# A fixed TensorE order by kind of product in the attention of a decoder layer, with folded maxima

## The chip, the core and the metric

The kernel runs on one core of a Trainium2 chip. A core has a matrix engine (TensorE, in profiles PE, with its weight loads as PEld), a vector engine (VectorE, DVE), a scalar engine for activations (ScalarE, ACT), a general engine (GpSimd, POOL) and a queue engine that issues DMAs (SyncE, SP). Each works through its own list of instructions in the order in which the program was built, and waits on semaphores for the others. TensorE writes its products to a memory of its own, PSUM, that is divided into banks; DVE and ACT read them from there. Everything else is in SBUF or in DRAM.

The metric is the device time of one execution in microseconds. A profile is one such execution, recorded instruction by instruction.

## What is computed

One decoder layer on x of shape (16, 256, 256): pre-norm self-attention with 16 heads of 16 channels, pre-norm mLSTM cross attention with 8 heads of 32 channels against a context, and a mixture of experts (top 2 of 8). Cut to what matters here:

```
h = layernorm(x)
qkv = einsum('bsd,ndh->bnsh', h, W_qkv);  q, k, v = split(qkv, 3)
attn = softmax(q k^T / sqrt(16) + causal mask);  out = attn v
x = x + einsum('bds,nhd->bsd', out.reshape(B, 256, S), W_out)     # a reordering with a scale

q = layernorm(x);  k = v = ctx                                    # mLSTM
pre = 15 tanh((concat(q, k, v) @ ifgate_w.T + ifgate_b) / 15)
log_d = cumulated log_sigmoid(forget) differences + input gate, causal
d = exp(log_d - rowmax(log_d))
s = (q k^T / sqrt(32)) * d
h = s v / (max(|rowsum(s)|, exp(-m)) + 5e-5)
x = x + rms_normed(h) * gain

h = layernorm(x)
probs = softmax(h @ router_w + router_b);  two experts a token
x = x + sum over the two of  prob * gelu(h @ up_e^T) @ down_e^T
```

All data is float32.

## The kernel before

**Attention.** It goes through 16 sequences b, each in four quads of four heads: a round k = 4 b + quad. For a round:

- `maxima(k)`: eight row-group products (a contraction of 16 channels, one head in each group of 32 rows of TensorE's array) put the scores into two PSUM tiles of two banks, `ps_s`. The DVE subtracts the causal mask's blocks (`less`, line 371), takes the maxima of the rest (`off`, 375), reduces `less` (376), joins `off` (377) and transposes (380). Four small DMAs write the row maxima into a spare row of `qt`, so that the next product subtracts them.
- `weights(k)`: eight row-group products with a contraction of 32 give the shifted, transposed scores in two more such tiles, `ps_st` (398, 402); ACT exponentiates them into `p` (406), POOL zeroes the upper triangle (341).
- `values(k)`: eight column-group products (the heads lie beside each other in the output's partitions, 417, 422) into `ps_av`; ACT copies it to `avt`.
- by sequence: `start1` (layer norm on DVE, ACT and POOL), `turn1` (four transposes, whole array), `project` twice and `project_v` (whole array, 309 and 329), `by_token` (eight transposes into two tiles `ps_o`, 435, which the DVE scales into `av`, 440 to 442).

`attend_next(k)` calls maxima(k), turn1 or a projection of the next sequence, weights(k - 2), values(k - 4), project_v, by_token, start1. The tiles of maxima, weights and of the mLSTM's scores share one pool of three pairs of banks, `ps_p`; everything else of whole-array and column-group products shares two single banks, `ps_t`.

**The mLSTM beside it.** From round k0 = 36 on, when eight sequences are through, `take_evenly` calls between two rounds some five steps of a list that `mixing(0, False)` and `reorder(0)` made: `gather` and `spread` (transposes that reorder the attention's output), `load2`, `start2`, `turn2` (transposes of context and x), `gates` (32 column-group products, then a chain on ACT and DVE), `gates_by_token` (transposes of its result), `maxima2`, `decay` (ACT's exponentials, POOL's triangle), `scores2` (row groups into `ps_p`, the DVE multiplies by `d`, 618), `values2` (column groups, 632), `finish` (transposes and the norm), `layer3`, `scale3`, `turn3`, `logits`, `softmax3`, `choose`, `count`, and `send`, POOL's scatter of rows to the experts' table.

**What sets the order.** Up to the experts, a scheduler puts each engine's instructions in order by a model of their times when the program is built; the calls above only give their priorities. It splits groups: where it thinks that a slot is not free yet, it takes a product from another group first. The experts' part, from line 1187 on, stands under `tc.manual_schedule(engines={PE, ACT, SP})`, where those engines keep the order of the calls; the second half of the mLSTM is interleaved there by the same steps.

Of the kernel before, what the change touches and what calls it, by code (L numbers as in the profile page):

```python
# [12 lines left out]
F32 = mybir.dt.float32  # L13
# [7 lines left out]
P = 128  # L21
# [8 lines left out]
GB = 8  # L30
# [39 lines left out]
def decoder_layer(  # L70
# [35 lines left out]
    def xtile(b, c):  # L106
# [15 lines left out]
        out=mask_a, in_=mask_a, compare_op=ALU.is_ge, fill=1e10, base=0,  # L122
        pattern=[[0, SC], [-1, P]], channel_multiplier=1,
    )
    gain = const.tile([P, D], F32, name="gain")
    wrout_sb = const.tile([P, DC, E], F32, name="wrout_sb")
    brout_sb = const.tile([P, E], F32, name="brout_sb")
# [32 lines left out]
    def statistics(b, mv, rstd):  # L160

        for c in range(SC):
            st = lstm.tile([P, 6], F32, tag="st", name="st", bufs=4)
            nc.vector.bn_stats(st, xtile(b, c))
            nc.vector.bn_aggr(mv[:, c, :], st)
        nc.vector.tensor_scalar(rstd, mv[:, :, 1], LN_EPS, None, ALU.add)
        nc.scalar.activation(rstd, rstd, AF.Ln)
        nc.scalar.activation(rstd, rstd, AF.Exp, scale=-0.5)

    def normalized(xn, b, mv, rstd, engine=nc.gpsimd):  # L170
# [103 lines left out]
            nc.vector.tensor_reduce(wq[:, c, :], wsel, AX.X, ALU.add)  # L274

    def step(f, *args):
        return lambda: f(*args)

# [67 lines left out]
    def maxima(k):  # L346

        b, quad = divmod(k, NQ)
        qt, kt, mx = seq[b]["qt"], ks[b % 2], mxs[k % 2]

        ps = [ps_p.tile([P, 2, 512], F32, tag="s", name="ps_s") for _ in range(2)]

        def channels(h):
            return slice(HP * h, HP * h + HA)

        for h in range(4):
            nc.tensor.matmul(  # L357
                ps[h // 2][:, h % 2, P : P + S], lhsT=qt[channels(h), quad, P:], rhs=kt[channels(h), quad, :],
                start=True, stop=True,
            )  # L360
        for h in range(4):
            nc.tensor.matmul(  # L362
                ps[h // 2][:, h % 2, :P], lhsT=qt[channels(h), quad, :P], rhs=kt[channels(h), quad, :P],
                start=True, stop=True,
            )

        less = att.tile([P, 4, SC, P], F32, tag="less", name="less", bufs=1)
        off = att.tile([P, 4], F32, tag="off", name="off")
        for j, p in enumerate(ps):
            part = slice(2 * j, 2 * j + 2)  # L370
            nc.vector.tensor_tensor(  # L371
                less[:, part], mask_a[:, None].to_broadcast([P, 2, SC, P]),
                p.rearrange("p h (c k) -> p h c k", c=SC)[:, :, :, :P], ALU.subtract,
            )
            nc.vector.tensor_reduce(off[:, part], p[:, :, P:S], AX.X, ALU.max)  # L375
        nc.vector.tensor_reduce(mx[:, :, :4].rearrange("p c h -> p h c"), less, AX.X, ALU.min)  # L376
# [32 lines left out]
    def values(k):  # L409

        b, quad = divmod(k, NQ)
        p, v = quads[k]["p"], vs[b % 2]
        if quad == 0:
            seq[b]["avt"] = att.tile([P, NQ, S], F32, tag="avt", name="avt", bufs=1)
# [12 lines left out]
        del quads[k]  # L427
# [550 lines left out]

    avs = {}

    def attend_next(k):
# [12 lines left out]
        if 0 <= k - 4 < B * NQ:  # L994
            done, part = divmod(k - 4, NQ)
            if done % GB == 0 and part == 0:
                avs[done // GB] = big.tile([P, SC, HA, GB, NA], F32, tag="av", name="av")
            values(k - 4)
        if b + 1 < B and quad == NQ - 1:
            project_v(b + 1)  # L1000
        if 0 <= k - 4 < B * NQ and part == NQ - 1:
            by_token(done)
        if quad == NQ - 2 and b + 2 < B:
            start1(b + 2)

    for b in range(2):
        start1(b)
    turn1(0)
    for i in range(2):
        project(0, i)  # L1010
    project_v(0)
    output_sums()
    nc.vector.tensor_scalar(gain, gain, 1.0, None, ALU.add)
    k0 = GB * NQ + 4
    last = B * NQ + 4

# [33 lines left out]
    gathers, spreads = reorder(1)  # L1050
    for f in gathers:
        f()
    attention.close()
    singles.append(ctx.enter_context(tc.tile_pool(name="ps_s", bufs=6, space=PSUM)))

# [215 lines left out]
```

## Time and profile before

| | us |
|---|---|
| three executions: median | 1269.7 |
| lowest, highest | 1261.93, 1269.94 |
| the profiled execution | 1278.24 |
| its span, first to last instruction | 1276.5 |

Its mean granted TensorE clock is 0.906 of full speed. The costliest groups are the experts' products (lines 1140 and 1158, 271.1 and 265.5 us); of the attention, in microseconds of busy time:

| line | engine, what | count | busy | mean ns |
|---|---|---|---|---|
| 357 | PE, maxima, 256 columns | 512 | 84.0 | 443 |
| 398 | PE, weights, 256 columns | 512 | 79.3 | 462 |
| 309 | PE, project | 256 | 71.7 | 428 |
| 371 | DVE, less | 128 | 86.9 | 679 |
| 375 | DVE, off | 128 | 53.3 | 417 |
| 376 | DVE, reduce | 64 | 77.6 | 1212 |
| 618 | DVE, scores times d | 96 | 60.3 | 683 |
| 406 | ACT, exponential | 128 | 98.7 | 810 |
| 341 | POOL, triangle of p | 128 | 78.7 | 639 |

How to read it: the time of a PE row is the modelled time from a product's start to its end, and products of different row or column groups run beside each other, so their busy times overlap; the pitch, from the start of one group to that of the next, is what counts. Each float32 product of the program is two records. "[0.56 <-DVE off L375]" behind a row means that the engine was idle for 0.56 us before it, until the DVE's instruction of line 375 released it. The granted clock is the share of full TensorE speed that the chip's throttle gave.

### The profile page before, as it was taken

The numbers are of one execution on the slowest core, as the hardware profiler recorded it, in microseconds if no ns is written. First come the engines' busy times: TensorE is split into PE (matmuls) and PEld (weight loads), VectorE is DVE, ScalarE is ACT, GpSimd is POOL, SyncE is SP. The second block draws the span as 40 slices with busy tenths as digits, with TensorE's granted clock in tenths as the row PEclk, the third lists the DMA queues.
The fourth block names the chain that finished last, engine by engine and source line by source line (L and its number), as shares of the span: only waits on it lengthen the run. The fifth ranks groups of instructions, "written<-read, shape, count | busy, mean of one in ns | idle before, by whom it ended". The sixth has DMA issues, their size and how long they took to land. (4 is left out here: it accounts for less than half of the span.)

```text
span 1276.5 us, 23870 instructions
## 1 busy us (share of the span) xinstructions
PE 1137.2 (89%) x8962; PEld 879.5 (69%) x8962; DVE 611.9 (48%) x1660; ACT 460.6 (36%) x934; POOL 400.8 (31%) x449
## 2 busy tenths in 40 slices
PE   5999999989889998665898879999899999999993
PEld 4677777646656555344676647877678999999992
DVE  4788777767667557253458544564411111111110
ACT  2344444336546453122575316633211111111110
POOL 5233332345433334614121053201732112221121
PEclk9699999879889787686899969999979999999997
DMA  5200000003112100243675536635569788888825
GB/s 183 60 15 17 13 17 13 10 10 138 31 38 98 43 18 18 96 173 125 232 244 167 183 114 216 195 120 163 166 208 375 238 267 270 267 264 271 272 55 148
DMA packets 63410, 177.14 MB, mean 139 GB/s; under 512 B 11776, under 2 KB 43520, under 8 KB 48128
## 3 DMA queue, kind: packets, MB, share of 16 engines
q1 hardware_dynamic: 49072, 155.75, 35.0%
q0 software_dynamic: 13680, 19.08, 7.4%
q8 instruction: 72, 1.18, 0.4%
q10 hardware_dynamic: 544, 0.79, 0.2%
q14 instruction: 42, 0.34, 0.1%
HBM read 147.19 MB, written 28.13 MB: 137 GB/s over the span
## 5 line engine op out<-in xcount | busy, mean ns | idle before, releaser
L1140 PE MATMUL ps_u<-xt,up 128*128 128x128 f32 (+1 forms) x1632 | 271.1, 323 | 5.9 <-issue 4.2
L1158 PE MATMUL ps_d<-down,h 128*128 128x256 f32 x1136 | 265.5, 389 | 3.8 <-issue 3.4
L1140 PEld LDWEIGHTS ps_u<-xt,up 128*128 128x128 f32 x1632 | 240.3, 194 | 32.0 <-issue 11.4
L1158 PEld LDWEIGHTS ps_d<-down,h 128*128 128x128 f32 x1136 | 216.9, 195 | 38.8 <-issue 10.4
L1163 POOL DMA_INDIRECT acc<-y,to x71 | 110.2, 1553 | 392.9 <-DVE y L1162 316.1
L1146 ACT ACTIVATE h<-ps_u 128x512 f32<-128x512 f32 x84 | 50.2, 597 | 248.8 <-PE ps_u L1140 213.2
L341 POOL TENSOR_SCALAR_AFFINE_SELECT p<-p 128x512 f32<-128x512 f32 x128 | 78.7, 639 | 191.1 <-ACT p L406 146.3
L406 ACT ACTIVATE p<-ps_st 128x768 f32<-128x768 f32 x128 | 98.7, 810 | 91.8 <-PE ps_st L402 89.6
L371 DVE TENSOR_TENSOR less<-mask_a,ps_s 128x512 f32<-128x512 f32 x128 | 86.9, 679 | 43.3 <-PE ps_s L362 43.2
L1120 DVE COPY xt<-ps_r 128x256 f32<-128x256 f32 (+1 forms) x51 | 26.9, 527 | 145.4 <-PE ps_r L1118 126.5
L357 PE MATMUL ps_s<-kt,qt 16*128 16x256 f32 x512 | 84.0, 443 | 10.2 <-DVE d L618 6.3
L398 PE MATMUL ps_st<-qt,kt 32*128 32x256 f32 x512 | 79.3, 462 | 13.9 <-DVE off L375 12.7
L1162 DVE TENSOR_SCALAR y<-ps_d,wt 128x256 f32<-128x256 f32 x71 | 34.0, 478 | 110.0 <-PE ps_d L1158 95.3
L813 POOL DMA_INDIRECT table<-x,place x64 | 63.5, 991 | 64.3 <-DVE place L809 19.6
L376 DVE TENSOR_REDUCE mxs<-less 128x8 f32<-128x1024 f32 x64 | 77.6, 1212 | 0.0
L309 PE MATMUL ps_qk<-xnt,wqk_sb 128*128 128x256 f32 x256 | 71.7, 428 | 5.6 <-DVE wg_in L488 2.7
L341 POOL TENSOR_SCALAR_AFFINE_SELECT d<-d 128x512 f32<-128x512 f32 x64 | 40.6, 681 | 105.6 <-ACT d L600 90.0
L172 POOL TENSOR_SCALAR xn<-x,mv,rstd 128x256 f32<-128x256 f32 x46 | 56.6, 1240 | 43.7 <-PE ps_t L181 27.8
L618 DVE SCALAR_TENSOR_TENSOR d<-ps_sc,d 128x384 f32<-128x384 f32 (+1 forms) x96 | 60.3, 683 | 14.8 <-PE ps_sc L613 7.4
L600 ACT ACTIVATE d<-mb,at 128x256 f32<-128x256 f32 x128 | 63.8, 499 | 9.6 <-DMA mb<-mm 9.6
L1148 DVE COPY h<-ps_u 128x512 f32<-128x512 f32 x58 | 39.8, 688 | 52.0 <-PE ps_u L1140 34.1
L309 PEld LDWEIGHTS ps_qk<-xnt,wqk_sb 128*128 128x128 f32 x256 | 51.2, 210 | 17.5 <-issue 3.6
(220 smaller groups left out, 1652.8 us busy)
## 6 DMA issues: line engine op xcount, KB each, us to landing
up<-in_wup SPq DMA_DIRECT2D x51, 1024.0 KB
down<-in_wdown SPq DMA_DIRECT2D x51, 1024.0 KB
mb<-mm SPq DMA_DIRECT2D x16, 1024.0 KB
rows<-table SPq DMA_DIRECT2D x20, 265.0 KB
rows<-table SPq DMA_DIRECT2D x31, 132.5 KB
x<-in_x SPq DMA_DIRECT2D x16, 256.0 KB
kt<-qt SPq DMA_DIRECT2D x128, 32.0 KB
qt<-rowed SPq DMA_DIRECT2D x256, 1.0 KB
```

Of the source, the lines that this page charges most:

```text
L309: nc.tensor.matmul(ps[:, i, :], lhsT=wqk_sb[:, dc, n : n + 4].rearrange("p n j h -> p (n j h)"), rhs=xnt[:, dc, :], start=dc == 0, stop=dc ...
L341: nc.gpsimd.affine_select(out=block, in_=block, compare_op=ALU.is_ge, fill=0.0, base=0, pattern=[[0, 4], [1, P]], channel_multiplier=-1,)
L357: nc.tensor.matmul(ps[h // 2][:, h % 2, P : P + S], lhsT=qt[channels(h), quad, P:], rhs=kt[channels(h), quad, :], start=True, stop=True,)
L371: nc.vector.tensor_tensor(less[:, part], mask_a[:, None].to_broadcast([P, 2, SC, P]), p.rearrange("p h (c k) -> p h c k", c=SC)[:, :, :, : ...
L376: nc.vector.tensor_reduce(mx[:, :, :4].rearrange("p c h -> p h c"), less, AX.X, ALU.min)
L398: nc.tensor.matmul(ps[h][:, :S], lhsT=kt[rows(h), quad, :P], rhs=qt[rows(h), quad, :], start=True, stop=True)
L406: nc.scalar.activation(p[:, part, :], x_, AF.Exp, scale=1.0 / math.sqrt(HA))
L600: nc.scalar.activation(d[:, h, :S], mb[:, n, :], AF.Exp, bias=at[:, 0, j, n : n + 1], scale=-1.0)
L813: i = nc.gpsimd.indirect_dma_start(out=table, out_offset=bass.IndirectOffsetOnAxis(ap=place, axis=0), in_=row, in_offset=None, bounds_chec ...
L1140: nc.tensor.matmul(ps[:, j, :], lhsT=m["up"][:, dc, f * P : (f + 1) * P], rhs=m["xt"][:, dc, :t], start=dc == 0, stop=dc == DC - 1,)
L1158: nc.tensor.matmul(ps, lhsT=m["h"][:, f, c * P : (c + 1) * P], rhs=m["down"][:, f, :], start=f == 0, stop=f == FC - 1)
L1163: a = nc.gpsimd.indirect_dma_start(out=acc, out_offset=bass.IndirectOffsetOnAxis(ap=m["to"][:, c : c + 1], axis=0), in_=y, in_offset=None, ...
```

## The change

It does five things.

1. `attend_next` no longer calls the work at once. It sorts it into four slots: 0 holds maxima (row groups) and the mLSTM's loads, norms, `maxima2`, `decay` and `scores2`; 1 holds the whole-array products (turn1, project, project_v, by_token) and those steps that have no place of their own; 2 holds weights (row groups); 3 holds values (column groups) with `values2`, `gates`, `logits`, `layer3`, `scale3`. The steps of a sequence stay in their order, as do the steps that belong to none. The slots are then called one after the other.
2. The attention, from its first step on, stands under `tc.manual_schedule(engines={PE})`: TensorE keeps the order of the calls. The other engines are still ordered by the scheduler. The mLSTM's steps of a round are handed to `attend_next` with it instead of being called behind it.
3. values runs three rounds behind maxima instead of four; project_v and by_token come ahead of weights; `start1` is called one quad earlier.
4. In `maxima`, the block behind the diagonal is no longer reduced to `off`; a scalar_tensor_tensor folds it into `less` (min of -p and less), and the one reduce that follows covers it.
5. The layer norms' epsilon is added as the bias of ACT's logarithm instead of by a DVE operation (48 of them), and the context's transposes in `turn2` are copied from PSUM by ACT instead of the DVE.

The diff, cut to its core:

```diff
@@ statistics
-        nc.vector.tensor_scalar(rstd, mv[:, :, 1], LN_EPS, None, ALU.add)
-        nc.scalar.activation(rstd, rstd, AF.Ln)
+        nc.scalar.activation(rstd, mv[:, :, 1], AF.Ln, bias=ln_eps[:, 0:1])
@@ maxima
-            nc.vector.tensor_reduce(off[:, part], p[:, :, P:S], AX.X, ALU.max)
+            nc.vector.scalar_tensor_tensor(
+                less[:, part, 1], p[:, :, P:S], -1.0, less[:, part, 1], ALU.mult, ALU.min
+            )
         nc.vector.tensor_reduce(mx[:, :, :4].rearrange("p c h -> p h c"), less, AX.X, ALU.min)
-        nc.vector.scalar_tensor_tensor(mx[:, 1, :4], off, -1.0, mx[:, 1, :4], ALU.mult, ALU.min)
@@ turn2
-        nc.vector.tensor_copy(m["ct"], ps)
+        nc.scalar.copy(m["ct"], ps)
@@ attend_next
+    def attend_next(k, also=()):
+        slots = [[], [], [], []]
         b, quad = divmod(k, NQ)
         if k < B * NQ:
-            maxima(k)
+            slots[0].append(step(maxima, k))
         if b + 1 < B:
             if quad == 0:
-                turn1(b + 1)
+                slots[1].append(step(turn1, b + 1))
             elif quad < NQ - 1:
-                project(b + 1, quad - 1)
+                slots[1].append(step(project, b + 1, quad - 1))
+            else:
+                slots[1].append(step(project_v, b + 1))
+        if quad == NQ - 1 and 0 < b <= B:
+            slots[1].append(step(by_token, b - 1))
+        if quad == 1 and b + 2 < B:
+            slots[0].append(step(start1, b + 2))
         if 0 <= k - 2 < B * NQ:
-            weights(k - 2)
+            slots[2].append(step(weights, k - 2))
...
+        if 0 <= k - 3 < B * NQ:
+            slots[3].append(step(values, k - 3))
+        at, least = {}, 0
+        for f, *args in also:
+            own = 1
+            if f in (load2, start2, maxima2, decay, scores2):
+                own = 0
+            elif f in (values2, logits, gates, layer3, scale3):
+                own = 3
+            if f in by_sequence:
+                own = at[args[0]] = max(own, least, at.get(args[0], 0))
+            else:
+                own = least = max([own, least, *at.values()])
+            slots[own].append(step(f, *args))
+        for f in sum(slots, []):
+            f()
@@ the loops
-    for k in range(k0):
-        attend_next(k)
+    with tc.manual_schedule(engines={PE}):
+        ...
+        for k in range(k0):
+            attend_next(k)
...
-    for k in range(k0, last):
-        attend_next(k)
-        take_evenly(steps, k + 1 - k0, last - k0 - EARLY)
+    with tc.manual_schedule(engines={PE}):
+        for k in range(k0, last):
+            done = min(all_steps, all_steps * (k + 1 - k0) // (last - k0 - EARLY))
+            n = max(0, done - (all_steps - len(steps)))
+            attend_next(k, [f.work for f in steps[:n] if f is not None])
+            steps = steps[n:]
```

More of the change, by code (lines that the diff above doesn't have):

```diff
@@ L124, in decoder_layer @@
     )
+    ln_eps = const.tile([P, 1], F32, name="ln_eps")
+    nc.gpsimd.memset(ln_eps, LN_EPS)
     gain = const.tile([P, D], F32, name="gain")
@@ L276, in step, with run @@
     def step(f, *args):
-        return lambda: f(*args)
+        def run():
+            f(*args)
+        run.work = f, *args
+        return run
     seq, quads = {}, {}
@@ L367, in maxima @@
         less = att.tile([P, 4, SC, P], F32, tag="less", name="less", bufs=1)
-        off = att.tile([P, 4], F32, tag="off", name="off")
         for j, p in enumerate(ps):
@@ L413, in values @@
         if quad == 0:
+            if b % GB == 0:
+                avs[b // GB] = big.tile([P, SC, HA, GB, NA], F32, tag="av", name="av")
             seq[b]["avt"] = att.tile([P, NQ, S], F32, tag="avt", name="avt", bufs=1)
@@ L979, in decoder_layer @@
     avs = {}
-    def attend_next(k):
+    def attend_next(k, also=()):
+        slots = [[], [], [], []]
         b, quad = divmod(k, NQ)
         if k < B * NQ:
-            maxima(k)
+            slots[0].append(step(maxima, k))
         if b + 1 < B:
             if quad == 0:
-                turn1(b + 1)
+                slots[1].append(step(turn1, b + 1))
             elif quad < NQ - 1:
-                project(b + 1, quad - 1)
-        if 0 <= k - 2 < B * NQ:
-            weights(k - 2)
[L994 to L1013, printed above, removed]
+                slots[1].append(step(project, b + 1, quad - 1))
[5 more added lines that the diff above has]
+            slots[0].append(step(start1, b + 2))
+        if 0 <= k - 2 < B * NQ:
+            slots[2].append(step(weights, k - 2))
[15 more added lines that the diff above has]
+            f()
+    by_sequence = (load2, start2, turn2, maxima2, decay, scores2, values2, finish, layer3, scale3, turn3, logits)
     k0 = GB * NQ + 4
@@ L1025, in take_evenly @@
             take(steps)
-    for k in range(k0):
-        attend_next(k)
+    with tc.manual_schedule(engines={PE}):
+        for b in range(2):
+            start1(b)
+        turn1(0)
+        for i in range(2):
+            project(0, i)
+        project_v(0)
+        output_sums()
+        nc.vector.tensor_scalar(gain, gain, 1.0, None, ALU.add)
+        for k in range(k0):
+            attend_next(k)
     tail = NBLK - THIRD
@@ L1046, in decoder_layer @@
     all_steps = len(steps)
-    for k in range(k0, last):
-        attend_next(k)
-        take_evenly(steps, k + 1 - k0, last - k0 - EARLY)
-    gathers, spreads = reorder(1)
-    for f in gathers:
-        f()
+    with tc.manual_schedule(engines={PE}):
[4 more added lines that the diff above has]
+            steps = steps[n:]
+        gathers, spreads = reorder(1)
+        for f in gathers:
+            f()
     attention.close()
```

## The prediction, made before the changed kernel ran

> **What bounds the kernel now.** I read the page first, then the windows by stage, then TensorE's timeline in one period of each stage, then the DVE's beside it.
>
> From the page:
>
> ```profile
> span 1276.5 us, 23870 instructions
> PE 1137.2 (89%) x8962; PEld 879.5 (69%) x8962; DVE 611.9 (48%) x1660; ACT 460.6 (36%) x934; POOL 400.8 (31%) x449
> PE   5999999989889998665898879999899999999993
> PEclk9699999879889787686899969999979999999997
> ```
>
> TensorE is the busy engine from slice 2 to the end, but its granted clock sags in the middle. By stage (columns: window, length, busy of PE, PEld, DVE, ACT, POOL, clock, DMA share, GB/s):
>
> ```profile
> 67.00:250.00 183.00, 175.92 (x1956) 129.59 (x1948) 141.14 (x317) 83.28 (x152) 56.82 (x80) 0.99 0.06 14
> 250.00:500.00 250.00, 229.06 (x2276) 146.72 (x2274) 162.07 (x360) 129.04 (x319) 105.35 (x126) 0.86 0.15 49
> 500.00:546.00 46.00, 32.20 (x231) 20.66 (x232) 17.88 (x82) 10.38 (x25) 25.37 (x28) 0.57 0.24 83
> 546.00:940.00 394.00, 333.42 (x2313) 258.01 (x2312) 202.44 (x618) 164.69 (x312) 116.88 (x116) 0.89 0.52 174
> ```
>
> The plain attention (67 to 250) is bound by TensorE at full clock. The mixed stage (attention with the mLSTM, 250 to 500) has 20.9 us of idle TensorE and, at 0.86, loses about 0.14 x 250 = 35 us to the clock. Behind 546 the order is written out by hand already; what happens earlier shifts it as a whole. The change acts before 546.
>
> TensorE in one plain period, quads 3 and 0:
>
> ```profile
> 104.39 0.88 PE L357 MATMUL ps_s<-kt,qt 16*128 16x256 f32 x8
> 105.27 0.70 PE L398 MATMUL ps_st<-qt,kt 32*128 32x256 f32 x4
> 106.53 0.48 PE L398 MATMUL ps_st<-qt,kt 32*128 32x256 f32 x2 [0.56 <-DVE off L375]
> ...
> 110.00 0.60 PE L435 MATMUL ps_o<-ident,avt 128*128 128x128 f32 x4
> 110.53 0.69 PE L357 MATMUL ps_s<-kt,qt 16*128 16x256 f32 x2
> 111.15 0.66 PE L435 MATMUL ps_o<-ident,avt 128*128 128x128 f32 x4
> ```
>
> Two losses are seen: `weights` finds the third PSUM pair only, and waits for the DVE to empty the first pair of `maxima`; and one row-group product alone between two groups of transposes takes 111.15 - 110.53 = 0.62 us, where eight together take 0.88. The DVE at that time:
>
> ```profile
> 105.36 0.69 DVE L371 TENSOR_TENSOR less<-mask_a,ps_s 128x512 f32<-128x512 f32 x1 [1.00 <-PE ps_s L362]
> 105.97 0.42 DVE L375 TENSOR_REDUCE off<-ps_s 128x2 f32<-128x256 f32 x1
> 106.30 0.68 DVE L371 TENSOR_TENSOR less<-mask_a,ps_s 128x512 f32<-128x512 f32 x1
> 107.23 1.21 DVE L376 TENSOR_REDUCE mxs<-less 128x8 f32<-128x1024 f32 x1
> ```
>
> **The change, part by part.** Pitches (start to start, full clock) from this timeline: maxima 0.9, half a projection 1.92, `project_v` 1.83, four transposes 0.55 to 0.6, weights 0.87, values 0.78.
>
> *Plain stage.* Quads 1 and 2 keep their order: 4.5 us each (115.58 to 120.08), no change. Quad 3 with quad 0 now takes 115.58 - 104.39 = 11.19 us. New order: maxima, `project_v`, eight transposes, weights, values; then maxima, four transposes, weights, values. In the built order the DVE works less, less, fold, fold, reduce. A fold is an operation the trace lacks on this tile; its nearest rows are the reduce it replaces (0.42) and the scalar_tensor_tensor on 128x384 of ps_sc (0.55), so 0.42. The first PSUM pair is then free 0.60 + 0.60 + 0.42 + 0.14 = 1.8 us after maxima, not 1.25. Quad 3: `project_v` and the transposes (3.3 us, with 0.3 for ACT to empty ps_v) hide that; but values needs the slot of the first ps_o, which the DVE empties only behind its maxima work: less and fold 1.95, reduce 1.24, reciprocal 0.29, transpose 0.26, product 0.21, the second reciprocal 0.29, `av` 0.60, semaphore 0.14: 5.0 us after maxima, where TensorE is there at 3.3 + 0.87 = 4.17. Quad 3 is 0.95 + 5.0 + 0.79 = 6.75. Quad 0: four transposes do not cover 1.8 us, so weights ends 1.8 + 0.85 (106.53 to 107.38, what follows the wait) after maxima: 0.95 + 2.65 + 0.79 = 4.4. Sum 11.15 against 11.19: the wait of 0.56 and the lone product are gone, and two waits on the DVE take their place. Nine sequences: 0 us at full clock. The folded maxima save the DVE a 0.17 us operation and its 0.04 gap a round: off the path.
>
> *Mixed stage, removed.* About 25 lone products as at 110.53, 0.62 - 0.11 each: -12.5 us. Waits of weights for the DVE (12.7 us between 20 and 520, nine of 0.56 in the plain stage): -8.
>
> *Mixed stage, added.* `scores2` now follows maxima at once, both row groups, three PSUM pairs for four: its second half waits for the DVE's fold, 1.8 us instead of 0.3: about 1.5 us, 14 times, +21, less the 6 us that maxima now waits for `d`: +15. Three rounds have two sets of scores, and the second waits also for the first `d` behind the reduce (4.3 us after maxima; 0.95 us a `d`): +2 each, +6. In four quad-3 rounds `finish` follows the transposes of `by_token` and waits for both ps_o slots: +6 in all; values behind ps_o in the others, +3. `gates`: from its last product (277.45) to the transposes of its rows (286.04) the chain on ACT and DVE, a reciprocal of 3.35 us in it, takes 8.6 us; now 2.9 us of products stand between, and TensorE holds weights, values and everything behind: +3, the second unit +1. `count`: logits' transpose at 499.84, its product at 509.16, with 1.9 us idle; nothing stands between any more: +5. Sum of the stage: -20.5 + 39 = +18.
>
> *Values one round sooner.* weights, two exponentials (1.5), two selections on POOL (1.22): 3 us, with 3.2 to 5.7 us until values. POOL's other pieces are 2.4 us. I put 0; if POOL stands in the way in a third of 28 rounds, +10. *Order of sums, start:* maxima of quad 0 no longer stand behind the second sequence's projection and its 2.66 us of waiting for wg_in: -2 (0 to -5). *eps as bias:* 48 DVE operations of 0.21 us gone, off TensorE's path in the attention; *ct on ACT* (0.58 instead of 0.69 us on the DVE): in the mixed stage ACT is busy 129 of 250 us and empties in turn, 0.1 us a transpose; behind 546 TensorE waits 11.6 us for the DVE's ct, 10.8 of it once, and ACT could stand behind a gelu instead. Both together -2 (-8 to +6).
>
> *The clock.* A row speaks against the new waits:
>
> ```profile
> 238.57 0.60 PE L398 MATMUL ps_st<-qt,kt 32*128 32x256 f32 x2 [0.98 <-DVE off L375]
> ...
> 241.39 2.39 PE L329 MATMUL ps_v<-wv_sb,xnt 128*128 128x256 f32 x8
> ```
>
> After an idle 0.98 us the same product runs at half speed (2.39 for 1.99, 0.70 for 0.41) for some 4 us, so such a gap costs 2 us more; gaps of 0.77 (415.11) and 0.76 (476.75) do the same, nine gaps of 0.56 never did. The Trainium skill ("TensorE: Matmul & The Clock Gate", "Why this matters for your kernels") asks only that gaps stay under about 3 us; by it no new wait but those of gates and count costs clock, and the sum is +14. By the row, the gap before values in quad 3 (0.76 in the trace's way of counting) may cost 2 us in each of nine sequences: half of them, +9, of which I take +5; in the mixed stage I let new gaps and removed ones cancel. I follow the row. Sum: 0 + 5 + 18 - 2 - 2 = +19 us.
>
> The profiled execution took 1278.2 us (span 1276.5 and 1.7 around it), 0.7% above the median of 1269.7; I add the sum to the median: **1288 us**.
>
> **The rivals.**
> 1. *Faster: the clock stays up.* Place: 250 to 500. With four blocks a round, TensorE may see no short gaps, and most of the 35 us of clock comes back beside the lone products' 12.5. For: nine of the eleven falls that the timeline shows between 260 and 500 follow a wait of a row-group product for the DVE. Against: scores behind maxima. It decides from a clock of 0.95 in that stage on (0.09 x 250 = 22 us back): -12.5 - 22 = -35: 1235 and lower.
> 2. *No change: the stage follows its chain of evacuations.* DVE's 5.3 us for a maxima and a scores set, and ACT beside it, set the rounds before and after: removed and added waits are equal: 1270.
> 3. *Much slower: the clock falls in every round.* Each 1.5 us gap before scores costs 2 us more (14 x 2), and both waits in all nine plain sequences (36): 1288 + 28 + 31 = about 1345 at the most, 1315 by half.
> 4. *POOL holds values:* +10, 1298; the lag is what it needs.
> 5. *The order is not what TensorE gets:* excluded, the built program has it.
>
> **How the numbers follow.** Forecast with rival 4: 0.46 (1275 to 1305); rival 3: 0.10; rival 2: 0.19; rival 1: 0.25. Less than 1% (12.7 us) is about what a measurement can tell from no change. Faster by over 1%: 0.25; within: 0.20, some of the forecast's lower end among it; slower: 0.55. The range reaches into rival 1 and rival 3: 1235 to 1318; the slower cases alone 1275 to 1318.
>
> **What would show it.** Right: quads 3 and 0 together near 11.1 us, with TensorE waiting for a fold in quad 0 and for the DVE's `av` in quad 3; waits of `scores2` for folds of over 1 us, a dozen of them; a wait of 4 us or more behind gates and behind the logits' transposes; mixed stage 15 to 20 us longer at a clock of 0.8 to 0.88. Wrong: clock of the mixed stage at 0.95; lone-product savings with no wait before scores; values waiting for POOL as the longest wait; or a gain or loss of over 10 us behind the attention.

## The result and the profile after

| | before | after |
|---|---|---|
| median of six executions each, us | 1269.09 (1261.93 to 1272.76) | 1333.84 (1332.1 to 1340.39) |
| span of the profiled one, us | 1276.5 | 1331.9 |
| its mean granted TensorE clock | 0.906 | 0.889 |

The ratio of the medians is 1.0524, with a 95% interval of 1.0489 to 1.0559. The forecast was 1288: the sign was right, the size (+19 us) was a third of what came (+65), and the time lies above the range, which reached to 1318.

The page of the kernel after, the lines that answer to those shown of before:

```profile
span 1331.9 us, 23756 instructions
...
PE 1112.4 (84%) x8962; PEld 876.2 (66%) x8962; DVE 582.2 (44%) x1532; ACT 474.6 (36%) x950; POOL 400.0 (30%) x450
...
PE   5989999767777767656589887999989999999993
...
PEclk8999999766887878768689887999979999999997
```

TensorE's busy time is 24.8 us *less* than before (1137.2), at a lower mean clock. The loss is idle TensorE, 84% busy for 89%, and it stands in slices 8 to 17, of 33 us each. By stage (columns as before; the windows are moved with the stages, the last two by 56 us):

```profile
67.00:243.00 176.00, 164.13 (x1887) 122.72 (x1885) 127.93 (x267) 80.24 (x144) 53.25 (x76) 0.98 0.07 14
243.00:556.00 313.00, 221.30 (x2269) 151.50 (x2264) 155.86 (x342) 136.24 (x331) 110.75 (x130) 0.78 0.12 40
556.00:602.00 46.00, 31.98 (x245) 20.41 (x246) 12.69 (x53) 11.38 (x23) 23.21 (x26) 0.61 0.22 77
602.00:996.00 394.00, 332.00 (x2317) 258.84 (x2316) 195.74 (x594) 170.75 (x320) 116.81 (x116) 0.89 0.53 173
```

In the mixed stage TensorE is busy 221 us of 313; before it was 229 of 250. Where the time went, by the first and last starts that the trace gives for each tile:

| us | before | after | difference |
|---|---|---|---|
| start to the first transposition of `turn2` | 251.7 | 243.7 | -8.0 |
| from there to the last maxima (mixed stage) | 250.0 | 320.5 | +70.5 |
| from there to the experts' first product | 66.0 | 60.8 | -5.2 |
| from there to the last one's start | 677.2 | 675.0 | -2.2 |

The second milestone does not stand at quite the same place in both: in round 40 `turn2` comes 6.4 us behind the start of the maxima before, and 1.6 us after. So some 5 us of the -8.0 and of the +70.5 are this shift alone.

Two places of the mixed stage, TensorE's timeline and then VectorE's. First a set of scores behind maxima:

```profile
355.33 0.71 PE L362 MATMUL ps_s<-kt,qt 16*128 16x256 f32 x8
...
356.08 0.60 PE L616 MATMUL ps_sc<-qt,ct 32*128 32x256 f32 x4
360.19 0.48 PE L616 MATMUL ps_sc<-qt,ct 32*128 32x256 f32 x2 [3.51 <-DVE less L379]
...
361.05 1.11 PE L182 MATMUL ps_t<-ident,xn 128*128 128x128 f32 x4
```

```profile
353.14 0.69 DVE L678 TENSOR_TENSOR sq<-ps_hn,g 128x512 f32<-128x512 f32 x1 [1.03 <-ACT g L677]
357.58 0.75 DVE L166 BATCH_NORM_STATS2 st<-x 128x6 f32<-128x256 f32 x2 [3.74 <-POOL x L682]
...
358.46 1.25 DVE L375 TENSOR_TENSOR less<-mask_a,ps_s 128x512 f32<-128x512 f32 x2
359.63 0.75 DVE L379 SCALAR_TENSOR_TENSOR less<-ps_s,less 128x256 f32<-128x256 f32 x2
```

The second half of `scores2` waits 3.51 us for the fold of line 379. That fold is not late because it is long. In VectorE's queue the statistics of the next layer norm (line 166) stand ahead of `less`, and they wait 3.74 us for GpSimd to finish the mLSTM's `x`. TensorE was through with these maxima by 356.3, but their banks come free only at about 360.

Then the end of the stage, where the experts' rows are counted:

```profile
556.02 0.69 PE L802 MATMUL ps_n<-sel,earlier 128*128 128x64 f32 x2 [9.63 <-DVE sel L789]
556.50 3.10 PE L802 MATMUL ps_n<-sel,ones 128*128 128x56 f32 x14
...
559.96 1.24 PE L403 MATMUL ps_st<-qt,kt 32*128 32x256 f32 x8
...
561.55 1.08 PE L424 MATMUL ps_av<-p,v 128*32 128x256 f32 x8
```

TensorE stands for 9.63 us in front of `count`, while VectorE works through the choice of experts; weights, values and the next maxima, which need nothing of it, are queued behind. Afterwards the clock is at half: eight records of weights take 1.24 us, not 0.71.

### The profile page after: what moved, and what is told of

The parts are those of the page before. It is cut to its first block, busy times and chain, and to the rows that moved or that the text cites. A ratio compares the mean times of both kernels' runs of the same rounds, so it can differ in the third digit from the quotient of the medians.

```text
span 1331.9 us, 23756 instructions
## 1 busy us (share of the span) xinstructions
PE 1112.4 (84%) x8962; PEld 876.2 (66%) x8962; DVE 582.2 (44%) x1532; ACT 474.6 (36%) x950; POOL 400.0 (30%) x450
## 5 line engine op out<-in xcount | busy, mean ns | idle before, releaser
L1184 PE MATMUL ps_d<-down,h 128*128 128x256 f32 x1136 | 262.0, 386 | 4.3 <-issue 4.1
L375 DVE TENSOR_TENSOR less<-mask_a,ps_s 128x512 f32<-128x512 f32 x128 | 82.1, 681 | 114.7 <-PE ps_s L367 113.6
L314 PE MATMUL ps_qk<-xnt,wqk_sb 128*128 128x256 f32 x256 | 82.9, 481 | 0.7 <-ACT xnt L301 0.7
L362 PE MATMUL ps_s<-kt,qt 16*128 16x256 f32 x512 | 61.0, 448 | 15.8 <-ACT p L411 9.5
L607 ACT ACTIVATE d<-mb,at 128x256 f32<-128x256 f32 x128 | 63.6, 497 | 18.8 <-DMA mb<-mm 14.5
L314 PEld LDWEIGHTS ps_qk<-xnt,wqk_sb 128*128 128x128 f32 x256 | 58.2, 238 | 14.9 <-issue 1.5
L403 PE MATMUL ps_st<-qt,kt 32*128 32x256 f32 x512 | 63.0, 495 | 4.3 <-DVE less L379 3.9
L616 PE MATMUL ps_sc<-qt,ct 32*128 32x256 f32 x256 | 38.1, 475 | 33.2 <-DVE less L379 22.4
L625 DVE SCALAR_TENSOR_TENSOR d<-ps_sc,d 128x384 f32<-128x384 f32 (+1 forms) x96 | 60.6, 677 | 11.6 <-POOL d L346 8.6
```

The costliest lines, as they stand in the source:

```text
L314: nc.tensor.matmul(ps[:, i, :], lhsT=wqk_sb[:, dc, n : n + 4].rearrange("p n j h -> p (n j h)"), rhs=xnt[:, dc, :], start=dc == 0, stop=dc ...
L362: nc.tensor.matmul(ps[h // 2][:, h % 2, P : P + S], lhsT=qt[channels(h), quad, P:], rhs=kt[channels(h), quad, :], start=True, stop=True,)
L375: nc.vector.tensor_tensor(less[:, part], mask_a[:, None].to_broadcast([P, 2, SC, P]), p.rearrange("p h (c k) -> p h c k", c=SC)[:, :, :, : ...
L403: nc.tensor.matmul(ps[h][:, :S], lhsT=kt[rows(h), quad, :P], rhs=qt[rows(h), quad, :], start=True, stop=True)
L607: nc.scalar.activation(d[:, h, :S], mb[:, n, :], AF.Exp, bias=at[:, 0, j, n : n + 1], scale=-1.0)
L1184: nc.tensor.matmul(ps, lhsT=m["h"][:, f, c * P : (c + 1) * P], rhs=m["down"][:, f, :], start=f == 0, stop=f == FC - 1)
```

## The experiments

The executions were taken on several chips. On some the kernel before takes about 1268 us, on others about 1229, nearly all of the difference behind the experts' first product (677 and 636 us from there). So each run is read by its ratio to the kernel before on its own chip, and by the lengths of its stages. An expectation in microseconds that was written for 1269 is read by its difference from before.

**The edits apart.** Four kernels: the small edits without the order, the order without the small edits, and two that give the mixed stage's TensorE back to the scheduler.

```diff
 small_alone: before, with folded maxima, bias=ln_eps, and nc.scalar.copy(m["ct"], ps)
 order_alone: after, with those three taken back
 mixed_by_scheduler: after, with
-    with tc.manual_schedule(engines={PE}):
+    if True:
         for k in range(k0, last):
 plain_fixed_only: after, with
+    for k in range(k0, last):
+        attend_next(k)
+        take_evenly(steps, k + 1 - k0, last - k0 - EARLY)
```

> The kernel before with only the three small edits (folded maxima, LN's constant as ScalarE's bias, turn2's ct copied by ScalarE) and TensorE's order left to the scheduler. Theory A (the added time is TensorE's fixed order in the mixed stage, which waits for evacuations that VectorE and ScalarE reach late): within 8 us of before, 1262 to 1277. Theory B (the small edits did it: first half of the maxima's banks freed 0.6 us later, ScalarE loaded with more): 1300 or more.

> The changed kernel with the three small edits taken back: only the order is fixed (values a round earlier with it). Theory A: the cost stays, 1320 to 1345 (the folded maxima shorten VectorE's chain by about 0.7 us in 26 rounds of the mixed stage at most, so undoing them may add up to 15). Theory B: 1290 or less.

> The changed kernel, but the mixed stage is not under TensorE's fixed order: the steps are called in the same slots and the scheduler orders TensorE as it did before. Theory A (the fixed order itself, which cannot move scores2 or a transposition behind other work when its bank is not free): 1260 to 1285, the first count 45 us or more after the mixed stage's start earlier than in the changed kernel. Theory C (the order in which the slots call the steps is what costs, since the scheduler of the other engines follows it too): 1315 or more.

> The changed kernel up to round 36 (fixed order, which reached the mixed stage 8 us before the kernel before did); in the mixed stage the steps are dealt out behind each round as before and the scheduler orders TensorE. Theory A: 1258 to 1268, the 8 us kept and nothing lost behind it. Theory D (what follows the mixed stage, where the changed kernel took 10 us more from its first count to its first expert product, has its own cost, from values a round earlier or from ct on ScalarE): 1268 to 1282.

Measured, beside the two kernels on chips of the faster kind (before_look and after_third, described below):

| | ratio to before (95%) | mixed stage reached at | its length |
|---|---|---|---|
| before_look | 1 | 246.8 | 254.1 |
| after_third | 1.048 (1.042 to 1.055) | 244.4 | 312.4 |
| small_alone | 1.030 (1.026 to 1.034) | 281.1 | 251.5 |
| order_alone | 1.024 (1.021 to 1.028) | 225.3 | 300.7 |
| mixed_by_scheduler | 1.015 (1.012 to 1.019) | 244.8 | 270.6 |
| plain_fixed_only | 1.0015 (0.999 to 1.004) | 254.7 | 249.7 |

Neither A nor B is the whole. The small edits alone cost 3%, all of it ahead of the mixed stage. The order alone costs 2.4%, but it is a gain of 21 us up to the mixed stage and a loss of 47 in it. The gain, from the starts of the rounds: 5 us ahead of the first maxima (20.8 for 25.7), 7 in the rounds 0 to 35 (174.6 us for 182.0), 4 in the next four, and 5 that are only the earlier place of `turn2`. With the small edits in, the loss is 58 us. Of it the scheduler takes back 42 (312.4 to 270.6). The dealing out behind each round makes the stage shorter by another 21 (249.7), but that stage begins 10 us later (254.7 for 244.8), so 11 us are gained by its end. The order of the calls costs too, as C has it, but less than TensorE's fixed order.

How the small edits cost 34 us of plain attention (the copy of ct is not in it), by windows (20 to 60 us is the start; then the plain stage). The kernel with the small edits alone, then the one with the order alone:

```profile
20.00:60.00 40.00, 36.82 (x190) 24.48 (x190) 19.87 (x45) 9.24 (x18) 9.70 (x10) 0.56 0.19 54
60.00:220.00 160.00, 152.43 (x1537) 111.17 (x1538) 105.92 (x213) 66.64 (x118) 48.80 (x68) 0.93 0.06 14
```

```profile
20.00:60.00 40.00, 37.77 (x374) 27.17 (x377) 32.84 (x84) 15.91 (x32) 13.34 (x16) 0.91 0.22 60
60.00:220.00 160.00, 154.44 (x1846) 116.74 (x1843) 126.55 (x289) 78.68 (x142) 53.62 (x76) 1.00 0.07 16
```

In the same 160 us there are 1537 records of products against 1846, at a clock of 0.93 against 1.00. The timeline of small_alone:

```profile
107.10 0.48 PE L399 MATMUL ps_st<-qt,kt 32*128 32x256 f32 x2 [0.44 <-DVE less L375]
...
108.38 0.25 DVE L167 BATCH_NORM_AGGREGATE mv<-st 128x2 f32<-128x6 f32 x2 [1.09 <-POOL xn L173]
...
108.72 0.30 ACT L168 ACTIVATE rstd<-mv,ln_eps 128x2 f32<-128x2 f32 x1 [2.29 <-DVE mv L167]
...
109.16 1.49 ACT L407 ACTIVATE p<-ps_st 128x768 f32<-128x768 f32 x2
...
110.01 0.48 PE L358 MATMUL ps_s<-kt,qt 16*128 16x256 f32 x2 [0.57 <-ACT p L407]
...
111.25 3.78 PE L310 MATMUL ps_qk<-xnt,wqk_sb 128*128 128x256 f32 x8
```

weights waits 0.44 us for the fold. In VectorE's queue the norm's `mv` (line 167) has come to stand ahead of the maxima's reduction, and waits 1.09 us for GpSimd's `xn`; with the order alone it stands behind that reduction and waits for nothing. ScalarE's Ln (line 168) needs `mv`, stands ahead of the exponentials, and waits 2.29 us. So `p` is late, the next maxima wait 0.57 us for a bank, and the projection behind them runs at half speed, 3.78 us for 1.99. At TensorE no link is as long as a microsecond.

**Which of the small edits, and two sides of the order.**

```diff
 without_bias: after, with
-        nc.scalar.activation(rstd, mv[:, :, 1], AF.Ln, bias=ln_eps[:, 0:1])
+        nc.vector.tensor_scalar(rstd, mv[:, :, 1], LN_EPS, None, ALU.add)
+        nc.scalar.activation(rstd, rstd, AF.Ln)
 without_fold: after, with
+            nc.vector.tensor_reduce(off[:, part], p[:, :, P:S], AX.X, ALU.max)
 plain_order_bare: plain_fixed_only without the three small edits
 scores_later: after, with
-            if f in (load2, start2, maxima2, decay, scores2):
+            if f in (load2, start2, maxima2, decay):
```

> The changed kernel with the layer norm's constant added by VectorE again (folded maxima and ct on ScalarE stay). The small edits alone had cost 3%, all of it before round 36 (mixed stage reached at 281.1 us, before: 251.7), and with the order fixed they cost 18 us there (243.7 against 225.3). Theory E (the layer norm's Ln, now behind VectorE's mv alone, stands in ScalarE's queue ahead of the exponentials while VectorE is late, and the next maxima then find their banks taken): without it the mixed stage is reached 15 us or so earlier than with all edits (near 226), ratio to before 1.03 to 1.04. Theory F (the folded maxima free the first pair of banks 0.6 us later): nothing gained there, mixed stage at 241 to 246, ratio 1.05.

> The changed kernel with the maxima reduced as before (off apart; the bias and ct on ScalarE stay). Theory F: mixed stage reached near 226, ratio 1.03 to 1.04, and TensorE's waits for the last reader of the maxima gone from weights and smaller at scores2. Theory E: mixed stage at 241 to 246, ratio 1.05.

> The fixed order up to round 36 without the three small edits, and the mixed stage dealt out as before under the scheduler. If the two parts are what they look like alone (the plain stage 26 us shorter with the bare order, the fixed order in the mixed stage 35 us longer than under the scheduler), this is faster than the kernel before by about 26 us: ratio 0.975 to 0.985. If the scheduler's mixed stage gives it back (it starts with other work left over), 0.99 to 1.0.

> The changed kernel with scores2 in the slot of the whole-array products, behind them, instead of directly behind the maxima. Theory A1 (scores2's second pair of banks waits for VectorE's last read of the maxima, 22.4 us in 11 waits, and the clock falls behind such waits): mixed stage 15 to 30 us shorter, ratio 1.03 to 1.04. Rival A2 (the time goes with VectorE's and ScalarE's late evacuations as a whole, and another product waits in its place): within 8 us of the changed kernel, ratio 1.045 to 1.06.

| | ratio (95%) | mixed stage reached at | its length |
|---|---|---|---|
| without_bias | 1.026 (1.023 to 1.029) | 232.2 | 304.9 |
| without_fold | 1.015 (1.013 to 1.018) | 227.9 | 300.2 |
| plain_order_bare | 0.9747 (0.973 to 0.977) | 231.0 | 239.1 |
| scores_later | 1.026 (1.023 to 1.029) | 245.6 | 300.8 |

E and F each hold a part, and neither is the whole: against the bare order (225.3) the bias alone adds 2.6 us (2.1 of them ahead of the first maxima), the fold alone 6.9, the two together 19 to 20. The place is quad 1, from the start of its maxima to that of the next. Over sequences 1 to 5 it takes 4.5 to 5.0 us with the bare order and without the fold, 5.1 to 6.0 without the bias, and 6.2 to 7.9 in the kernel after; in sequences 6 to 8 it takes 4.5 to 4.8 in all of them. Between 60 and 220 us, `mv` waits for GpSimd 6.5 us in four places in the kernel after, 6.4 without the bias, and not at all without the fold; the Ln then waits for VectorE 10.7 us, 2.8 and not at all. The fold changed VectorE's order, and the bias made ScalarE's Ln wait at just that spot. The third small edit, ct copied by ScalarE, shows no cost: without_fold keeps it and the bias, and its mixed stage is 300.2 us long, beside 300.7 with the bare order. (Its ratio even lies below order_alone's 1.024. The two reach the experts within about 2 us of each other, at 583.6 and 581.5, so the difference stands behind; it is not explained.)

Moving `scores2` takes 11.6 us off the mixed stage (312.4 on this kind of chip), less than A1 and more than A2 expected, though the ratio fell below A1's range: a part of the loss that can be named, not the bulk.

plain_order_bare is the version that beats both kernels: 1199.4 us where before takes 1231.3. Its start, its plain stage and its mixed stage, by windows:

```profile
20.00:60.00 40.00, 37.78 (x367) 27.19 (x369) 32.77 (x84) 15.63 (x31) 13.37 (x16) 0.91 0.21 60
60.00:220.00 160.00, 154.85 (x1854) 116.46 (x1847) 125.56 (x286) 78.98 (x142) 53.69 (x76) 1.00 0.07 16
231.00:470.10 239.10, 219.36 (x2274) 145.68 (x2274) 160.82 (x362) 128.22 (x318) 105.99 (x126) 0.87 0.16 53
```

Against before_look, 16 us of the gain stand ahead of the mixed stage (231.0 for 246.8) and 15 in it (239.1 for 254.1), where the scheduler orders TensorE in both. What made the latter shorter was not tested: its busy time is 219.4 us for 232.1, at a clock of 0.87 for 0.85. Set beside order_alone, which leaves out the same small edits, it shows what the fixed order of the mixed stage costs with its slots: 56 us by the stage's end (the last maxima at 526.0 and 470.1). Set beside plain_fixed_only, it shows that the small edits cost 2.7%. Every kernel with the new order also runs values three rounds behind maxima and calls `start1` a quad earlier; no run parts these from the order.

**Three mends of the mixed stage.**

```diff
 layer3_later: after, with
-        lags = ((1, scores2), *end, (5, layer3), (7, scale3), (8, turn3), (9, logits))
+        late3 = 0 if slow else 2
+        lags = ((1, scores2), *end, (5 + late3, layer3), (7 + late3, scale3),
+                (8 + late3, turn3), (9 + late3, logits))
 count_later: after, with a round's steps cut ahead of count where choose is among them, and kept for the next
 mixed_mended: order_alone with both of these, and scores2 as in scores_later
```

In layer3_later and mixed_mended, two of the sixteen sequences (1 and 2) get the router logits of the sequence behind them, so their tokens go to other experts; the engines' counts of instructions are those of the kernels that they were made from.

> The changed kernel itself on this chip, where the kernel before takes 1230 us instead of 1269, nearly all of the difference behind the first expert product. If the loss is in the attention and the mixed stage alone, as milestones say, it is the same 50 to 65 us here: ratio 1.042 to 1.053, mixed stage reached at 243 to 247, its length to the first count 305 to 315. If the two chips' clocks make the loss, it is smaller than 35 us.

> The changed kernel with the layer norm behind the mLSTM, and what follows it in a sequence (scale3, turn3, logits), two half-sequences later. Theory A4 (VectorE stands in that norm's statistics, waiting for GpSimd's x, with the maxima's evacuation queued behind it, and so TensorE waits 3.2 to 3.5 us at scores2's second pair in four places): those four waits fall to about 1.2 us, and the mixed stage is 8 to 15 us shorter, ratio about 0.01 below the changed kernel's. Rival A5 (the norm is only the last of several things VectorE waits for): no wait of over 3 us behind the norm, but others in its place, within 5 us.

> The changed kernel with the count of the experts' rows held back one round where the choice it depends on is made in the same round (once, at the end of the mixed stage, where TensorE waited 9.6 us for VectorE's choice with weights, values and maxima queued behind). Theory A6 (a chain of small VectorE operations ahead of a TensorE product costs its full length under a fixed order): TensorE's longest wait at the count falls below 3 us, and the time falls by 5 to 8 us. Rival: the count ends the mixed stage either way and the experts' first block starts from it, so that the time stays within 3 us.

> The bare fixed order in both stages (no folded maxima, no bias, ct on VectorE) with the three mends together: scores2 behind the whole-array products, the norm two half-sequences later, the count a round later. Plain stage as in the bare order: mixed stage reached at 225 to 228. Theory A (three nameable places make the fixed order's loss): mixed stage 245 to 260, as long as the scheduler's 247 to 258, ratio 0.975 to 0.99. Rival G (in a fixed order VectorE's and ScalarE's queues, still made by the scheduler, meet TensorE's at ever other places): 270 to 285, ratio 1.0 to 1.015.

| | ratio (95%) | mixed stage reached at | its length | experts' first product |
|---|---|---|---|---|
| after_again | 1.052 (1.045 to 1.060) | 243.5 | 320.5 | 624.8 |
| layer3_later | 1.045 (1.036 to 1.053) | 243.9 | 308.6 | 614.6 |
| count_later | 1.052 (1.044 to 1.060) | 247.0 | 306.4 | 624.7 |
| mixed_mended | 1.024 (1.017 to 1.032) | 226.8 | 295.9 | 587.0 |

layer3_later brought the experts forward by 10 us, but not as A4 said. VectorE does the statistics exactly where it did:

```profile
357.23 0.75 DVE L166 BATCH_NORM_STATS2 st<-x 128x6 f32<-128x256 f32 x2 [3.74 <-POOL x L682]
...
358.90 1.25 DVE L375 TENSOR_TENSOR less<-mask_a,ps_s 128x512 f32<-128x512 f32 x2
```

The call came two half-sequences later, and the scheduler, which still orders VectorE, put the work in the same place, with the same 3.74 us; the scores' waits for the fold are 25.4 us where they were 22.4. So the place of that norm in VectorE's queue was not tested.

count_later is the rival's case. The wait of 9.63 us falls to 4.6, and the last maxima come 11 us earlier, but the experts begin at 624.7 where it was 624.8. New waits stand behind the count: 9.0 us at `finish`, 5.8 at logits. What the count waits for ended no earlier.

mixed_mended keeps the bare order's plain stage, and its mixed stage is 296 us long: 5 less than with the bare order alone on a faster chip, and 46 more than the scheduler's on this kind. TensorE's waits in it are 75 us, of 84 with the bare order: those of the scores fell from 20.7 to 5.6 us, those for the transpositions' `ps_t` rose from 14.5 to 22.1. A fell; G said 270 to 285, and even that was too good.

**Whether the whole-array products' own banks set the pace**, with both kernels beside them on one chip.

```diff
 bare_scores_later: order_alone, with scores2 as in scores_later
 bare_spread: bare_scores_later, with
+            elif f in (turn2, finish, turn3):
+                own = 2
```

> The changed kernel itself, for the stage lengths beside the next three on one chip. If the loss is 62 to 66 us on any chip: ratio 1.049 to 1.054, and from the mixed stage's first transposition to the last maxima 315 to 325 us. If it depends on the chip: outside these.

> The fixed order in both stages without the three small edits, and scores2 behind the whole-array products. If the small edits (18 us before the mixed stage and some in it) and the place of scores2 (20 us) add up: mixed stage reached at 225 to 228, from there to the last maxima 275 to 290 us (before: 250), ratio 1.0 to 1.015. If the waits only move: 296 to 302 us as with the bare order alone or with three mends, ratio 1.02 to 1.03.

> As bare_scores_later, and in the mixed stage turn2, turn3 and finish stand behind weights, not beside attention's own whole-array products: the users of ps_t's two banks are parted by the row groups. Theory H (the grouping by kind lets one pair of banks' evacuations set the pace): waits for ps_t tiles fall by half, and the stage is 10 us or more shorter than bare_scores_later. Rival G (the queues of VectorE and ScalarE meet TensorE's at other places, whatever the grouping): within 5 us of it.

> The kernel before, for its stages on this chip: mixed stage reached at 250 to 253, from there to the last maxima 248 to 252. If the chip is one on which it takes 1230 us, the difference to 1269 lies behind the first expert product (630 to 640 us instead of 677).

For the mixed stage, the sums of the view of waits, which lists what TensorE's products waited for:

| | ratio (95%) | length | waits, us (times) | for ps_sc | ps_t | ps_st | busy | clock |
|---|---|---|---|---|---|---|---|---|
| before_look | 1 | 254.1 | 21.2 (25) | - | 4.0 | 4.9 | 232.1 | 0.85 |
| after_third | 1.048 (1.042 to 1.055) | 312.4 | 92.6 (55) | 31.0 | 14.9 | 0.3 | 219.6 | 0.80 |
| bare_scores_later | 1.016 (1.009 to 1.022) | 294.1 | 77.7 (53) | 10.6 | 16.3 | 4.5 | 216.3 | 0.82 |
| bare_spread | 1.017 (1.011 to 1.024) | 296.8 | 71.7 (62) | 11.4 | 4.6 | 11.0 | 224.9 | 0.79 |

after_third loses 61 us here, close to the 65 of the slower chip. In bare_scores_later the mends do not add up fully: its place of `scores2` is worth 6.6 us (300.7 to 294.1) where it was worth 11.6 with the small edits in.

bare_spread did to its waits what H said: those for ps_t fell from 16.3 to 4.6 us. The stage did not get shorter: weights' waits took half of that back (4.5 to 11.0), and at the lower clock the busy time is 8.6 longer. That is as G has it. The costliest waits of bare_scores_later in its mixed stage (total, times, longest):

```profile
PE ps_n L801 <- DVE sel L788: 9.7, 1, 9.7
PE ps_sc L615 <- DVE off L379: 8.8, 4, 3.0
PE ps_h L638 <- ACT avt L432: 5.1, 5, 1.5
PE ps_g L582 <- DVE a L563: 4.8, 1, 4.8
PE ps_st L402 <- DVE d L624: 4.5, 7, 1.2
PE ps_t L181 <- DVE mxs L381: 4.1, 1, 4.1
```

and of the kernel before on the same chip:

```profile
PE ps_s L357 <- DVE d L618: 6.3, 7, 2.4
PE ps_st L398 <- DVE off L375: 4.9, 8, 1.3
...
PE ps_g L576 <- DVE a L557: 1.8, 1, 1.8
```

No group of the former is over 10 us, and there are thirty of them. Under the scheduler there were 25 waits in all, and 21 us. A fixed order under which the other queues are fixed too, to fit it, was not tried.

## Why the prediction was wrong in size

Step by step, against the sum of +19 us (0 + 5 + 18 - 2 - 2):

- *Start, -2 (0 to -5):* right. The first maxima came at 22.9 us for 27.9 (23.7 for 25.7 on the chip of the last runs), and the clock between 20 and 60 us is 0.87 for 0.70 (0.91 with the bare order, 0.56 with the small edits alone).
- *Plain stage, 0, and +5 of clock:* near in sum, and that by luck. Quads 3 and 0 take 10.49 us (103.84 to 114.33), not 11.15. The wait for the fold in quad 0 came (0.51 us at 112.69). The wait for `av` did not: `av` is there about 4.2 us behind the end of maxima, where I had 5.0, and TensorE reaches values at about 4.4, where I had 4.17. (With the bare order it does wait there, 0.45 us in each of eight sequences, and the two quads take 10.24.) "Quads 1 and 2 keep their order: 4.5 us each" failed: quad 1 takes 6.2 to 7.9 us for 4.5 in five sequences. The maxima in it have a wait that I had not named, 1.09 us at 116.12, for the exponentials behind ScalarE's Ln, and behind three of the five waits the clock fell. The rounds 0 to 35 became 6 us longer (190.7 for 184.8), near my +5, because two errors cancel: on the faster chips the bare order makes these rounds 7 us shorter than before (174.6 for 182.0), and the small edits add 16.
- *Folded maxima 0, eps and ct -2 (-8 to +6):* this step failed. I had the first pair free at 1.8 us for 1.25, and charged it to one wait a sequence in the plain stage; and I called the 48 operations that the bias removes "off TensorE's path in the attention". What counted was neither duration: the two changed what waits for what in VectorE's and ScalarE's queues, and a wait for GpSimd came to stand ahead of the exponentials. Measured: 19 us up to the mixed stage and, by 312.4 against 300.7, some 12 in it.
- *Mixed stage, removed, -12.5 and -8:* the mechanism was right. No lone row-group product is left of some 25, and TensorE changes from one kind of product to another 93 times in the stage, for 189. What this saved cannot be read apart from the clock: the busy time fell by 12.5 us on the faster chip (232.1 to 219.6, clock 0.80 for 0.85), but by 0.3 us on the chip of the first pair (229.1 to 228.8, clock 0.77 for 0.86). In the stage weights waits 0.3 us for 4.9, on the faster chip.
- *Mixed stage, added, +39:* this step failed. On one chip the waits rise from 21.2 to 92.6 us, +71 net of what went away, where my terms for waits come to +31 net (39 less 8); busy fell by 12.5, and the difference of the two is about the 58 us by which the stage is longer (254.1 to 312.4). On the chip of the first pair it is longer by 70.5, for the 18 of my sum. By terms, in the table below: `scores2` was well sized, and `count` and `gates` were too small. What I left out is the other users of ps_t's two banks, 29 us: I had priced the banks that scores and maxima share, and taken those of the transpositions as free but for one place.
- *The clock in the mixed stage, "new gaps and removed ones cancel":* failed as well, 0.80 for 0.85 (0.77 for 0.86 on the chip of the first pair, where the lone products' gain does not show).
- *Behind 546, shifted as a whole:* right to 2 us from the experts' first product on; ahead of it 5 us came back.
- *Rivals:* 2 (the stage follows its evacuations) named the cause and had removed and added waits equal; they are not. 3 (clock) is a part. 1 is out: 0.80, not 0.95. 4 is out: up to the last maxima values never waits for GpSimd's `p`, and from there to the experts' first product once, 2.6 us (three times, 9.3 us, in after_third).
- *The clock by the row or by the page:* the Trainium skill's "Why this matters for your kernels" in "TensorE: Matmul & The Clock Gate" asks only that gaps stay under about 3 us. The row on short gaps was the better guide: in small_alone 0.44 and 0.57 us, 2.9 us apart, are followed by 3.78 us for 1.99. It was not exact either. Of the "nine gaps of 0.56" that "never did", the first, at 44.23 us and 1.9 us behind one of 0.48, is followed by half speed until 57. The +5 taken for the clock came to about 5 (quad 1 takes 7.9 for 6.2 us in three sequences), but behind another wait than the one it was taken for.

Added waits of the mixed stage, before_look against after_third:

| waits of | in the sum, us | measured, us |
|---|---|---|
| `scores2` | 27 | 31.0 (20.7 with the bare order) |
| `finish` and values behind `ps_o` | 9 | 2.4 |
| `gates` and its transposes | 4 | 6.0 (9.7, of which 3.7 were there before) |
| `count` | 5 | 9.6 |
| other transpositions into `ps_t` | 0 | 10.9 (14.9 for 4.0) |
| `values2` | 0 | 7.6 |
| `by_token` | 0 | 4.6 |
| values, behind other readers than `av` | 0 | 3.6 |
| `logits` | 0 | 2.4 |
| maxima | -6 | -2.2 (for `d` -3.6, for `p` +2.6, for `off` -1.2) |
| sum | 39 | 76 |

## What to carry to other kernels

A fixed order on one engine is only as good as the queues of the engines that empty its banks: if those are still ordered by an estimate, price the wait of every bank's user, not of the one pool that the change is about. Where the stage has one kind of work and a short period, fixing the order paid (16 us of 247 in plain_order_bare); where a second pipeline with long chains through VectorE, ScalarE and GpSimd ran beside it, the scheduler's order, with the work dealt out behind each round, was worth more than 50. An operation removed from an engine can leave a wait on another, so ask what stands behind the instruction that now waits, and try each small edit alone: two that cost 3 and 7 us cost 19 together.

## What the runs showed of the hardware that was not expected

How long a gap must be to cost TensorE its clock is not told by its length, nor by the gaps beside it. Eight of the nine gaps of 0.56 us in the kernel before cost nothing. In the kernel after, a pair of gaps of 0.51 and 1.09 us, 3.4 us apart, stands in four sequences (and one of 0.42 and 1.12 in the first), and the products behind the pairs take, in turn, 3.21, 1.99, 3.10, 1.99 and 3.00 us. Two neighbours, alike up to the projection:

```profile
89.73 0.48 PE L403 MATMUL ps_st<-qt,kt 32*128 32x256 f32 x2 [0.51 <-DVE less L379]
...
93.17 0.48 PE L362 MATMUL ps_s<-kt,qt 16*128 16x256 f32 x2 [1.09 <-ACT p L411]
...
94.02 3.10 PE L314 MATMUL ps_qk<-xnt,wqk_sb 128*128 128x256 f32 x8
...
112.69 0.48 PE L403 MATMUL ps_st<-qt,kt 32*128 32x256 f32 x2 [0.51 <-DVE less L379]
...
116.12 0.48 PE L362 MATMUL ps_s<-kt,qt 16*128 16x256 f32 x2 [1.09 <-ACT p L411]
...
116.97 1.99 PE L314 MATMUL ps_qk<-xnt,wqk_sb 128*128 128x256 f32 x8
```

after_third repeats it on another chip: 3.21, 1.99, 3.07, 1.99, 2.95. In small_alone the pair of 0.44 and 0.57 us cost clock in three sequences of four. What decides between them is not shown.

After both waits of over 3 us shown above the clock fell. Behind the one that ended at 360.19 it did so with a delay: the first products run at full speed (0.41 us), and from about 361 on at half (four transpositions 1.11 us, where 0.65 is full).
